# Message passing over 1.65 million edges on one core: some source rows fetched row by row on two other engines, and node transfers for four blocks

## The chip, the core and the metric

The kernel runs on one core of a Trainium2 chip. A core has five engines that take their own instructions in order: TensorE (PE in the profile; its weight loads are PEld), VectorE (DVE), ScalarE (ACT), GpSimd (POOL) and SyncE (SP), and 16 DMA engines that move data on their behalf. They meet through semaphores. The metric is the time of one execution on the device, in microseconds (us), lower being better.

## The reference

Nodes have 160 features (64 scalars, 32 vectors of three), edges four numbers; the edges are sorted by target.

```python
N, E = 50000, 1650000          # 2 x 800000 edges and a loop at each node
x   : [N, 160] f32             # node features
src, dst : [E] int32           # dst ascending
sh  : [E, 4] f32               # e0 = sh[:, :1], e1 = sh[:, 1:4]

s, v = x[:, :64], x[:, 64:].reshape(N, 32, 3)
ss, vv = s[src], v[src]                                        # gather of source rows
dot  = einsum('eui,ei->eu', vv, e1)
out0 = C0 * (ss * e0 @ W1 + dot * INV3 @ W2)
out1 = C1 * (p3 + p4 + p5)     # products of ss, vv with e0, e1 and W3, W4, W5
m    = concat([out0, out1])
h    = segment_sum(m, dst, N)  # then linear maps Ws, Wv
return layernorm(x + (x + relu(h)))
```

Every message is bilinear in the source's 160 features and the edge's four numbers, so the kernel first sums, for each target and each of the four edge numbers, the products with the source features, and applies the weights to the sums.

## The kernel before

**Units, groups, pairs.** The kernel takes most edges in units of 128. A unit needs the 128 source rows of `x` (640 bytes each), one on each partition: POOL fetches them with one indirect DMA (`gather`, L386) into a slot of `xg`. Six units are a group (`G`), three groups a "pair" of 18 units (`PG`), seven pairs a superchunk `s` (`SG` = 21 groups). `xg` has a tile for a pair, in four buffers, so POOL can be at most four pairs ahead of PE.

For each pair DVE makes `ha` (`spread`, L395 and L398): for each edge a one-hot of its target within a window of 32 nodes, times the four edge numbers, 128 x 128 a unit. PE multiplies `ha` by the unit's `xg` (`group_sums`, L423), six units adding up in one third of a PSUM tile `ps`. DVE turns `ps` over (`turn_sums`, L435) and adds the three groups into `ring` (L444), where a segment of four blocks of 128 nodes collects its sums. A kernel of 12,516 such units results.

**Blocks.** When the last group of a block of 128 nodes is past, PE multiplies its sums in `ring` by the weights (`block`, L756, five matmuls into `phb`), DVE adds relu of it to the node rows `xt` (L763) and takes mean and variance `mv` (L766, L768), ACT takes the root (`do_root`, L845, `rstd`), DVE inverts and applies it (`do_store`, L851 and L854), and SP stores the result (`do_send`, L862). `ahead` loads `xt` (L688). These steps come 1, 2, 3 and 4 pairs after the block's last group; two blocks (`BP`) share tiles and transfers.

**Own loops and packs.** The edges whose target is their source come as "own" rows in order of nodes (`ask_own`, L720 and L721, `set_own`). The others, without these, are rewritten to memory as `edges` in 16 `pack`s: DVE sorts out 128 long rows, and SP stores them row by row (`put`, L662), 18.9 KB of `edges` and 512 bytes of `selves` at addresses from registers, which one load of 16 numbers (L645) brings. `load` (L260) fetches a superchunk's edges on SP.

**Order.** SP, PE, DVE and ACT do things in the order in which the code is written (`manual_schedule`), and the loop over the pairs writes it: in each of the 18 unit steps of a pair it issues the unit's matmul, then `work(1.0)` takes waiting tasks from a queue that `after_pair` fills, then pack steps that are due. POOL has the gathers alone, in order.

Of the kernel before, what the change touches and what calls it, by code (L numbers as in the profile page):

```python
# [70 lines left out]
HEAD = 63  # L71
BP = 2
SB = 4
RP = 128
RS = 16
KM = 31
AHEAD = 3
SUMS = 3

def plan(n_nodes, n_edges):  # L80
# [24 lines left out]
def tile_gnn_resnorm(ctx: ExitStack, tc: tile.TileContext, x, src, dst, attr, W1, W2, W3, W4, W5, Ws, Wv, out, n_edges):  # L105
# [120 lines left out]
    with tc.tile_pool(name="once", bufs=1) as once, tc.tile_pool(name="raw", bufs=2) as rawp, \  # L226
            tc.tile_pool(name="idx", bufs=2) as idxp, tc.tile_pool(name="rows", bufs=4) as rowp, \
            tc.tile_pool(name="hots", bufs=1) as hotp, tc.tile_pool(name="ops", bufs=AHEAD + 1) as op, tc.tile_pool(name="sums", bufs=2) as sump, \
            tc.tile_pool(name="ring", bufs=2) as ringp, tc.tile_pool(name="node", bufs=6) as np_, \
            tc.tile_pool(name="ahead", bufs=6) as aheadp, \  # L230
            tc.tile_pool(name="psC", bufs=1, space=PSUM) as psC, tc.tile_pool(name="psK", bufs=1, space=PSUM) as psK, \
            tc.tile_pool(name="psP", bufs=1, space=PSUM) as psP, tc.tile_pool(name="psA", bufs=SUMS, space=PSUM) as psA, \
            tc.tile_pool(name="psM", bufs=1, space=PSUM) as psM, ExitStack() as later_pools:

        spotp, ownp = (later_pools.enter_context(tc.tile_pool(name=name, bufs=bufs))
                       for name, bufs in (("spot", 3), ("own", 2)))
        extremes = once.tile([P, 2, NSC], F32, name="extremes")
# [6 lines left out]
        nc.vector.tensor_copy(slotsP, slots)  # L244
        shareP, sumP = bank[:, 3, 64:64 + NK], bank[:, 3, 96:96 + BP * P // W]

# [3 lines left out]
        def load(s):  # L250
# [130 lines left out]

        def gather(s, placed, u, n):

            xg = rowp.tile([P, PG * G, D], F32, name="xg")
            for j in range(n):
                tc.add_to_no_dep_group(f"gathered{s % 2}", nc.gpsimd.indirect_dma_start(  # L386
                    out=xg[:, j, :], out_offset=None, in_=x,
                    in_offset=bass.IndirectOffsetOnAxis(ap=placed[0][:, u + j:u + j + 1], axis=0)).ins)
            return [xg[:, j, :] for j in range(n)]

# [27 lines left out]
        def group_sums(p, rows, ha):  # L418

            ps = psA.tile([P, PG, D], F32, name="ps")  # L420
            fresh("ps")
            for j, xr in enumerate(rows):
                mm = nc.tensor.matmul(ps[:, j // G, :], ha[:, j].rearrange("p k w -> p (k w)"), xr,  # L423
                                      start=j % G == 0, stop=j % G == G - 1)
                if j % G == 0:
                    wrote("ps", mm)
                else:
                    written["ps"][-1].append(mm.ins)
                yield ps

# [243 lines left out]
        def rows_of(b):  # L674
            nb = min(P, N - b * P)
            return nb, slice(b * P, b * P + nb)

        def together(b):

            bs = list(range(b // BP * BP, min(nblocks, b // BP * BP + BP)))  # L680
            return bs if all(rows_of(i)[0] == P for i in bs) else [b]

        def ahead(bs):

            nb = rows_of(bs[0])[0]
            n0, n1 = rows_of(bs[0])[1].start, rows_of(bs[-1])[1].stop
            xt = aheadp.tile([P, BP, D], F32, name="xt")
            dq.dma_start(xt[:nb, :len(bs)], x[n0:n1, :].rearrange("(h n) d -> n h d", h=len(bs)))  # L688

            mv = np_.tile([P, BP, 2], F32, name="mv")  # L690
            return [(xt, mv, h) for h in range(len(bs))]

# [7 lines left out]
        def own_blocks(k):  # L700

            if min((k + 1) * S, N) <= row_start(0)[1][0]:
                return []
            return [list(range(b, min(b + BP, nblocks))) for b in range(k * SB, min((k + 1) * SB, nblocks), BP)]

        def ask_own(k, bs, got):
# [5 lines left out]
            m = n // nq  # L712
            assert nq <= BP * P // W
            xr = ownp.tile([P, BP * P // W, D], F32, name="xr")
            sa = ownp.tile([P, BP * P // W, NK], F32, name="sa")
# [28 lines left out]

        products = {}

        def block(b, xt, mv, h):
            nb, row = rows_of(b)
            k, c0 = b // SB, b % SB * P
            bs = together(b)  # L750
            if b == bs[0]:
                products[b] = psM.tile([P, BP, D], F32, name="phb", tag="misc")
                fresh("misc")
            ph = products[bs[0]]
            for i in range(ND):
                wrote("misc", nc.tensor.matmul(ph[:nb, h], ring[k][:, i, c0:c0 + nb], BWk[:, i, :],  # L756
                                               start=i == 0, stop=i == ND - 1))
                yield 1
            if b != bs[-1]:
                return  # L760
            n = len(bs)
            y = xt[:nb, :n]
            nc.vector.scalar_tensor_tensor(y, ph[:nb, :n], 0.0, y, op0=ALU.max, op1=ALU.add)  # L763
            st = np_.tile([P, BP, 6], F32, name="st")
            for i in range(n):
                nc.vector.bn_stats(st[:nb, i], y[:, i])  # L766
            for i in range(n):
                nc.vector.bn_aggr(mv[:nb, i], st[:nb, i])  # L768

# [40 lines left out]
        def after_pair(p, f, *args):  # L810
            later.setdefault(p, []).append((f, args))
# [19 lines left out]

        def do_ahead(b):
            bs = together(b)
            if b == bs[0]:
                of_nodes.update(zip(bs, ahead(bs)))

        def do_block(b):
            yield from block(b, *of_nodes[b])

        def do_root(b):  # L840
            bs = together(b)
            if b == bs[-1]:
                n, (_, mv, _) = rows_of(b)[0], of_nodes[b]
                rstds[b] = np_.tile([P, BP], F32, name="rstd")
                nc.scalar.activation(rstds[b][:n, :len(bs)], mv[:n, :len(bs), 1], AF.Sqrt, bias=eps_t[:n])  # L845

        def do_store(b):
            bs = together(b)
            if b == bs[-1]:
                n, rstd = rows_of(b)[0], rstds.pop(b)  # L850
                nc.vector.reciprocal(rstd[:n, :len(bs)], rstd[:n, :len(bs)])  # L851
                for i in bs:
                    xt, mv, h = of_nodes[i]
                    nc.vector.tensor_scalar(xt[:n, h], xt[:n, h], mv[:n, h, 0:1], rstd[:n, h:h + 1],  # L854
                                            op0=ALU.subtract, op1=ALU.mult)

        def do_send(b):
            bs = together(b)
            if b == bs[-1]:
                n0, n1 = rows_of(bs[0])[1].start, rows_of(b)[1].stop  # L860
                xt = of_nodes[b][0]
                dq.dma_start(out[n0:n1, :].rearrange("(h n) d -> n h d", h=len(bs)), xt[:rows_of(b)[0], :len(bs)])  # L862
                for i in bs:
                    of_nodes.pop(i)

        def do_cast(s):
            raws[s] = cast(raws[s])

        def do_place(s):
# [72 lines left out]
        for b, g in enumerate(last_of):  # L942
            p = g // PG
            after_pair(max(p - 2, START - 1), do_ahead, b)
            for d, f in ((1, do_block), (2, do_root), (3, do_store), (4, do_send)):
                after_pair(p + d, f, b)
        later_pools.enter_context(tc.manual_schedule(engines={ET.SP, ET.PE, ET.DVE, ET.Activation}))
        turning = None
        for p, (s, g, ng) in enumerate(pairs):
            if p % per == 0 and s + 1 < NSC:  # L950
                end = reach(s + 1)
                assert end <= 0 or rows_stored[0] == NR or end <= row_start(rows_stored[0])[0][0]
                raws[s + 1] = load(s + 1)
                after_pair(p + 1, do_cast, s + 1)
# [3 lines left out]
            rows = gather(s, placed[s], (g - s * SG) * G, ng * G)  # L958
            for j, ps in enumerate(group_sums(p, rows, has.pop(p))):
# [194 lines left out]
```

## Time and profile before

| What | us |
|---|---|
| median of 3 runs | 17,977.61 |
| lowest and highest | 17,968.24, 17,986.82 |
| profiled execution | 18,051.88 |
| its span | 18,050.1 |
| POOL busy | 11,879.3 (66%) |
| DVE busy | 6896.5 (38%) |
| PE busy, matmuls | 6694.7 (37%) |
| PE busy, weight loads (beside the matmuls) | 5671.3 (31%) |
| ACT busy | 166.1 (1%) |

Times in the profile count from the span's start. A row of a group of instructions names the line, the engine, the operation, what it writes and reads, and the count, then busy time and the mean of one in ns, then the idle time just ahead of them on that engine and what ended most of it; "issue" means that nothing which the profile shows was waited for, and "remote" a releaser that it can't name. A row of the waits has total us, number and the longest. A row in order of time has start, duration, engine, line, operation and, in brackets, the idle time before. SPq and ACTq are the issuing of DMAs by SP and ACT. Register moves and loads are not shown as busy.

### The profile page before, as it was taken

The page shows a single profiled execution, that of the slowest core. Times are in us where ns is not written, and L with a number is a line of the kernel's source. Part 1 is how long each engine was busy: PE and PEld are TensorE (multiplying, and loading weights), DVE is VectorE, ACT ScalarE, POOL GpSimd, SP SyncE. Part 2 cuts the span into 40 slices and gives each one's busy share as a digit, 9 for nine tenths or more (in the row PEclk, how much of TensorE's full clock was granted, in tenths as well). Part 3 has the DMA queues.
Part 4 walks back from the last instruction along what each step waited for, and adds up shares of the span by engine and source line. Part 5 has one row for each costly group of instructions (what it writes and reads, how often), then busy time and mean ns, then how long its engine had stood idle before and what let it go on. Part 6 is the DMA issues. An engine that isn't in the chain of part 4 may idle for free. (4 is left out here: it accounts for less than half of the span.)

```text
span 18050.1 us, 95184 instructions
## 1 busy us (share of the span) xinstructions
PE 6694.7 (37%) x28959; PEld 5671.3 (31%) x28960; DVE 6896.5 (38%) x9751; ACT 166.1 (1%) x269; POOL 11879.3 (66%) x12530
## 2 busy tenths in 40 slices
PE   2333333333333333333333333333333333333333
PEld 2233333333333333333333333333233332333333
DVE  4343424334243343434334343343424434334222
ACT  0000000000000000000000000000000000000000
POOL 6566666666666666666666666666666666666666
PEclk6566566666666566566665666666666566656566
DMA  2223232222322323232232322323233232232222
GB/s 69 71 72 80 69 83 69 76 77 74 79 73 73 79 71 82 69 81 70 72 81 71 82 70 73 79 71 81 71 78 77 70 78 72 74 78 71 75 70 66
DMA packets 847363, 1343.26 MB, mean 74 GB/s; under 512 B 259593, under 2 KB 613844, under 8 KB 842784
## 3 DMA queue, kind: packets, MB, share of 16 engines
q0 software_dynamic: 600768, 1026.11, 23.9%
q1 hardware_dynamic: 244812, 310.13, 5.4%
q8 instruction: 230, 3.77, 0.1%
q14 instruction: 289, 2.37, 0.0%
q10 hardware_dynamic: 1264, 0.88, 0.0%
HBM read 1264.17 MB, written 72.09 MB: 74 GB/s over the span
## 5 line engine op out<-in xcount | busy, mean ns | idle before, releaser
L386 POOL DMA_INDIRECT xg<-in_x,sources x12516 | 11873.9, 949 | 6128.1 <-issue 3694.8
L423 PE MATMUL ps<-xg,ha 128*128 128x160 f32 x25032 | 5964.7, 365 | 8758.1 <-issue 8327.5
L423 PEld LDWEIGHTS ps<-xg,ha 128*128 128x128 f32 x25032 | 4955.5, 241 | 9606.1 <-issue 9123.2
L435 DVE STREAM_TRANSPOSE sums<-ps 128x480 f32<-128x480 f32 x696 | 469.7, 675 | 8745.5 <-PE ps L423 4451.9
L756 PE MATMUL phb<-BWk,ring 128*128 128x160 f32 (+1 forms) x3910 | 1225.8, 381 | 2522.0 <-issue 1747.7
L398 DVE TENSOR_TENSOR ha<-hot,pk 128x2304 f32<-128x2304 f32 x696 | 1776.1, 2552 | 24.9 <-DVE hot L395 1.0
L756 PEld LDWEIGHTS phb<-BWk,ring 128*128 128x128 f32 (+1 forms) x3910 | 882.3, 250 | 2694.7 <-issue 2358.5
L444 DVE TENSOR_TENSOR ring<-ring,sums 128x160 f32 x2086 | 688.0, 330 | 338.5 <-issue 232.6
L763 DVE SCALAR_TENSOR_TENSOR xt<-phb,xt 128x320 f32<-128x320 f32 x196 | 95.1, 485 | 1650.7 <-remote 1056.7
L395 DVE TENSOR_TENSOR hot<-bank,rel 128x576 f32<-128x576 f32 x696 | 521.4, 749 | 0.2
L740 DVE STREAM_TRANSPOSE ring<-xr 128x1280 f32<-128x1280 f32 x192 | 475.4, 2476 | 6.7
L610 DVE COPY_PREDICATED prow<-marks,prow 128x4734 f32<-128x4734 int32 (+6 forms) x80 | 432.7, 5409 | 0.6
L610 DVE COPY_PREDICATED pra<-marks,pra 128x3156 f32<-128x3156 int32 (+6 forms) x80 | 294.4, 3680 | 0.0
L736 DVE TENSOR_TENSOR xr<-xr,bank 128x1280 f32<-128x1280 f32 x192 | 284.8, 1483 | 10.2 <-remote 1.9
L845 ACT ACTIVATE rstd<-mv,eps_t 128x2 f32<-128x2 f32 x196 | 58.0, 296 | 17599.7 <-DVE mv L768 9083.3
L441 DVE TENSOR_TENSOR ring<-ring 128x199 f32<-128x199 f32 (+20 forms) x485 | 150.7, 377 | 2.3
L854 DVE TENSOR_SCALAR xt<-xt,mv,rstd 128x160 f32<-128x160 f32 x391 | 129.2, 372 | 15.2 <-issue 3.6
L698 DVE MEMSET ring<- 128x1255 f32 (+2 forms) x97 | 109.8, 1131 | 20.6 <-issue 20.6
L766 DVE BATCH_NORM_STATS2 st<-xt 128x6 f32<-128x160 f32 x391 | 108.2, 318 | 8.5 <-DVE xt L763 1.1
L368 DVE STREAM_TRANSPOSE pk<-raw 128x512 f32<-128x512 f32 x100 | 104.0, 1040 | 3.8 <-DMA raw<-in_attr 3.8
L607 DVE COPY_PREDICATED_SCALAR hit<-marks,none 128x789 int32 (+6 forms) x80 | 87.4, 1093 | 3.2 <-DVE pri L605 0.4
L627 DVE TENSOR_REDUCE mine<-pra 128x128 f32<-128x3200 f32 (+1 forms) x16 | 88.2, 5510 | 0.2
(337 smaller groups left out, 1469.9 us busy)
## 6 DMA issues: line engine op xcount, KB each, us to landing
xg<-in_x,sources POOLq DMA_INDIRECT x12516
xr<-in_x SPq DMA_DIRECT2D x191, 640.0 KB
edges<-prow SPq DMA_DIRECT2D x2030, 18.5 KB
raw<-edges SPq DMA_DIRECT2D x97, 384.0 KB
selves<-mine SPq DMA_DIRECT2D x2028, 0.5 KB
xt<-in_x SPq DMA_DIRECT2D x195, 160.0 KB
out<-xt SPq DMA_DIRECT2D x195, 160.0 KB
pra<-in_attr SPq DMA_DIRECT2D x15, 1580.0 KB
```

The source lines that it names most:

```text
L386: tc.add_to_no_dep_group(f"gathered{s % 2}", nc.gpsimd.indirect_dma_start(out=xg[:, j, :], out_offset=None, in_=x, in_offset=bass.Indirect ...
L395: nc.vector.tensor_tensor(hot[:, :n], slotsP[:, 0:W].unsqueeze(1).to_broadcast([P, n, W]), rel[:, u:u + n].unsqueeze(2).to_broadcast([P, n ...
L398: nc.vector.tensor_tensor(ha[:, :n], hot[:, :n].unsqueeze(2).to_broadcast([P, n, NK, W]), pk[:, :, u:u + n].rearrange("p k u -> p u k").un ...
L423: mm = nc.tensor.matmul(ps[:, j // G, :], ha[:, j].rearrange("p k w -> p (k w)"), xr, start=j % G == 0, stop=j % G == G - 1)
L435: nc.vector.transpose(at[:, :ng], ps[:, :ng].rearrange("p g (b f) -> p g b f", f=FB))
L441: nc.vector.tensor_tensor(ring[k][:, b, :past], ring[k][:, b, :past], ring[k - 1][:, b, S:S + past], op=ALU.add)
L444: nc.vector.tensor_tensor(here, here, at[:, i], op=ALU.add)
L610: nc.vector.copy_predicated(what[:n, a:e], mi[:, r].unsqueeze(2).to_broadcast([n, e - a, what.shape[2]]), what[:n, a + d:e + d])
L736: nc.vector.tensor_tensor(xr[:, :nq], xr[:, :nq], sumP[:, :nq].unsqueeze(2).to_broadcast([P, nq, D]), op=ALU.mult)
L740: nc.vector.transpose(ring[k][:, :, c0:c0 + nq * W].rearrange("p b (w q) -> p q b w", q=nq), xr[:, :nq].rearrange("p q (b f) -> p q b f", ...
L756: wrote("misc", nc.tensor.matmul(ph[:nb, h], ring[k][:, i, c0:c0 + nb], BWk[:, i, :], start=i == 0, stop=i == ND - 1))
L854: nc.vector.tensor_scalar(xt[:n, h], xt[:n, h], mv[:n, h, 0:1], rstd[:n, h:h + 1], op0=ALU.subtract, op1=ALU.mult)
```

## The change

Two engines take units from POOL. `ALONE` names for each: every how many pairs, at which remainder, and how many rows in a unit step. From pair 21 to pair 687 the second-last unit of every third pair is fetched by ACT and the last unit of every fourth pair by SP, each as 128 DMAs of one row of 640 bytes (`ask_alone`): eight loads of 16 addresses from `where` (which `address` makes on DVE once a superchunk) into registers, and for each row a register move and a DMA. Asking begins four pairs ahead (`LEAD`), three rows a unit step on ACT and two on SP. Their tiles have three buffers for each engine. The rows count up semaphores of their own, 16 for each engine, and PE waits for the whole unit just before its matmul. `gather` leaves these units out.

The other edits: `xt` and `out` move for four blocks in one DMA, 2560 contiguous bytes a partition in place of 640; a block's task does four blocks in two halves of two, with eight unit steps between; root, store and send come 3, 4 and 5 pairs after the last group. Own rows come for four blocks at once, in four DMAs of 32 partitions with four unit steps behind each. The edges of a superchunk are fetched in runs of 64 positions for two units each. `ha` is made two pairs ahead in place of three; the casts of a superchunk come in its third pair; fewer buffers for `xt` and own rows.

```diff
-BP = 2
+BP = 4
+AT = 2
+REST = 8
-AHEAD = 3
+AHEAD = 2
+ALONE = {"sync": (4, 1, 2), "scalar": (3, 0, 3)}
+LEAD = 4
+SEMS = 16
+AT_ONCE = 16
...
-                rows = what.rearrange("(u i q) -> i u q", u=P, i=NK)
-                dq.dma_start(to, rows)
+                rows = what.rearrange("(j i q) -> i j q", j=P // AT, i=NK)
+                dq.dma_start(to.rearrange("p (j t) q -> p j (t q)", t=AT), rows)
...
+        def address(s, at, fd, ef, af):
+            where = wherep.tile([P, NK, W], I32, name="where")
+            clipped = where.bitcast(F32)
+            nc.vector.tensor_scalar(clipped, ef[:, 0], 0.0, float(N - 1), op0=ALU.max, op1=ALU.min)
+            nc.vector.tensor_scalar(where, clipped, 4.0 * D, None, op0=ALU.mult)
+            where_of[s] = where, at[0]
+
+        def ask_alone(name, p):
+            s, g, ng = pairs[p]
+            where, u0 = where_of[s]
+            back = 1 + [n for n in ALONE].index(name)
+            u = u0 + (g - s * SG + ng) * G - back
...
+            to = alonep.tile([P, D], F32, name=f"alone_{name}")
+            sem, uses = kept[name][asked[name] % SEMS], asked[name] // SEMS + 1
...
+            came[p, back] = to, sem, uses * 16 * P, group
+            for i in range(NK):
+                for h in range(0, W, AT_ONCE):
+                    _, v = nc.values_load_multi_w_load_instructions(
+                        where[i * W + u // NK:i * W + u // NK + 1, u % NK, h:h + AT_ONCE], engines=[kind],
+                        min_val=0, max_val=(N - 1) * 4 * D, skip_runtime_bounds_check_because="clipped")
+                    for k in range(AT_ONCE):
+                        e = i * W + h + k
+                        d = eng.dma_start(to[e:e + 1, :].bitcast(U8), xbytes[ds(v[k], 4 * D)].rearrange("(o f) -> o f", o=1))
+                        d.then_inc(sem, 16)
...
+                        yield
...
             for j in range(n):
+                if n - j in alone:
+                    continue
...
+                alone = came.pop((p, len(rows) - j), None)
+                if alone:
+                    _, sem, count, group = alone
+                    tc.declare_fence(nc.tensor.wait_ge(sem, count).ins, group=group)
...
-            dq.dma_start(xt[:nb, :len(bs)], x[n0:n1, :].rearrange("(h n) d -> n h d", h=len(bs)))
+            dq.dma_start(xt[:nb, :len(bs)], x[n0:n1, :].rearrange("(n h) d -> n h d", h=len(bs)))
...
-                dq.dma_start(xr[:, :nq].rearrange("p q d -> p (q d)"), mine.unsqueeze(0).to_broadcast([NK, W, nq * D]))
                 dq.dma_start(sa[:, :nq].rearrange("p q k -> p (q k)"),
                              shares.unsqueeze(0).to_broadcast([NK, W, nq * NK]))
+                for part in range(NK):
+                    dq.dma_start(xr[part * W:(part + 1) * W, :nq].rearrange("p q d -> p (q d)"), mine)
+                    yield REST / 2
...
-            for d, f in ((1, do_block), (2, do_root), (3, do_store), (4, do_send)):
-                after_pair(p + d, f, b)
+                for d, f in ((1, do_block), (3, do_root), (4, do_store), (5, do_send)):
+                    after_pair(p + d, f, bs)
...
+        to_ask = {name: deque(p for p in range(3 * per, len(pairs) - 2 * LEAD) if p % every == at)
+                  for name, (every, at, _) in ALONE.items()}
...
                 work(1.0)
+                for name, of in to_ask.items():
+                    if name not in asking and of and of[0] - LEAD <= p:
+                        asking[name] = ask_alone(name, of.popleft())
+                    for _ in range(ALONE[name][2]):
+                        if name in asking and next(asking[name], 0) == 0:
+                            del asking[name]
```

The programs of three engines show where the rows stand. ACT before, from one pack to the next; `prow` and `marks` belong to the pack, `rstd` is the root of a block's variance, "x11" eleven instructions alike in a row:

```order
L526 CAST prow<-pri 128x790
L527 CAST prow<-pri 128x791
L528 COPY prow<-pra 128x790x4
L845 ACTIVATE rstd<-mv,eps_t 128x2
L546 CAST marks<-pri 128x790
L845 ACTIVATE rstd<-mv,eps_t 128x2 x11
```

ACT with the change, at the root of four blocks:

```order
L416 TENSOR_LOAD where
L421 DMA alone_scalar<-in_x 1x640 x14
L894 ACTIVATE rstd<-mv,eps_t 128x4 [waits DVE_49]
L421 DMA alone_scalar<-in_x 1x640 x2
L416 TENSOR_LOAD where
L421 DMA alone_scalar<-in_x 1x640 x16
```

Where ACT had a dozen instructions between packs, a root now stands behind and ahead of row DMAs.

SP before, while a pack is stored; the wait for DMAHW is that for the DMA eight ahead on SP, the wait for DVE that for the finished blocks:

```order
L662 DMA edges<-prow 1x18960 [waits DMAHW7_49]
L662 DMA selves<-mine 1x512 [waits DMAHW0_49]
L688 DMA xt<-in_x 128x2x160 [waits DMAHW1_49]
L862 DMA out<-xt 128x2x160 [waits DMAHW2_49,DVE_49]
L645 TENSOR_LOAD spots
L662 DMA edges<-prow 1x18960 [waits DMAHW3_49]
```

SP with the change, at such a place:

```order
L715 DMA edges<-prow 1x18960 [waits DMAHW0_49]
L715 DMA selves<-mine 1x512 [waits DMAHW1_49]
L906 DMA out<-xt 128x640 [waits DMAHW2_49,DVE_49]
L741 DMA xt<-in_x 128x640 [waits DMAHW3_49]
L416 TENSOR_LOAD where [waits DVE_49]
L421 DMA alone_sync<-in_x 1x640 [waits PE_sequencer_49,PE_49]
L421 DMA alone_sync<-in_x 1x640 x15
L416 TENSOR_LOAD where
L421 DMA alone_sync<-in_x 1x640 x4
L698 TENSOR_LOAD spots
L715 DMA edges<-prow 1x768 [waits DMAHW4_49]
```

The rows of `alone_sync` come between the stored rows, wait for no earlier DMA, and only the first for PE, which must be done with the buffer.

PE with the change, at the end of a pair whose last unit SP fetches (before, all 18 units of a pair read `xg` as the first rows do; DMASW is POOL's gathers):

```order
L474 MATMUL ps_141604<-xg_141586,ha_141036 128x160 [waits DMASW2_49]
L474 MATMUL ps_141604<-xg_141586,ha_141036 128x160 [waits DMASW3_49]
L474 MATMUL ps_141604<-alone_sync_140396,ha_141036 128x160 [waits own_sync13,PE_sequencer_49]
L474 MATMUL ps_141844<-xg_141825,ha_141404 128x160 [waits DMASW4_49,DVE_49,PE_49]
L474 MATMUL ps_141844<-xg_141825,ha_141404 128x160 [waits DMASW5_49]
```

Here PE stands until all 128 rows have landed, and the next pair's matmuls stand behind that.

More of the change, by code (lines that the diff above doesn't have):

```diff
@@ L388, in gather @@
                     in_offset=bass.IndirectOffsetOnAxis(ap=placed[0][:, u + j:u + j + 1], axis=0)).ins)
-            return [xg[:, j, :] for j in range(n)]
+            return [alone[n - j] if n - j in alone else xg[:, j, :] for j in range(n)]
         def spread(placed, u, n):
@@ L428, in group_sums @@
                     written["ps"][-1].append(mm.ins)
+                if alone:
+                    tc.declare_no_dep(mm.ins, group=group, reason="TensorE has waited for the semaphore of these rows")
                 yield ps
@@ L847, in do_store, with do_ahead @@
[L847 to L864, printed above, removed]
+        def do_ahead(bs):
+            of_nodes[bs[0]] = ahead(bs)
@@ L866, in do_cast, with do_send @@
+        def do_send(bs):
+            n0, n1 = rows_of(bs[0])[1].start, rows_of(bs[-1])[1].stop
+            xt, _ = of_nodes.pop(bs[0])
+            dq.dma_start(out[n0:n1, :].rearrange("(n h) d -> n h d", h=len(bs)), xt[:rows_of(bs[0])[0], :len(bs)])
         def do_cast(s):
             raws[s] = cast(raws[s])
+            address(*raws[s])
         def do_place(s):
@@ L957, in tile_gnn_resnorm @@
                     after_pair(p + 6, read_flags)
-            rows = gather(s, placed[s], (g - s * SG) * G, ng * G)
+            if p % per == 2 and s + 1 < NSC:
+                do_cast(s + 1)
+            rows = gather(s, placed[s], (g - s * SG) * G, ng * G, {b: came[p, b][0] for b in (1, 2) if (p, b) in came})
             for j, ps in enumerate(group_sums(p, rows, has.pop(p))):
```

103 lines of the change are left out of this document (56 added, 47 removed).

## The prediction

> **What bounds the kernel now.** I read the page first, then what GpSimd (POOL) waits for, then its gathers in order of time, and then the other engines in the same stretches. From the page:
>
> ```profile
> span 18050.1 us, 95184 instructions
> PE 6694.7 (37%) x28959; PEld 5671.3 (31%) x28960; DVE 6896.5 (38%) x9751; ACT 166.1 (1%) x269; POOL 11879.3 (66%) x12530
> L386 POOL DMA_INDIRECT xg<-in_x,sources x12516 | 11873.9, 949 | 6128.1 <-issue 3694.8
> L435 DVE STREAM_TRANSPOSE sums<-ps 128x480 f32<-128x480 f32 x696 | 469.7, 675 | 8745.5 <-PE ps L423 4451.9
> ```
>
> POOL does one thing, 12,516 gathers (L386), one for each unit of 128 edges. Its busy time and the idle time before it, 11,873.9 + 6128.1 = 18,002 us, fill the span, so the program lasts as long as POOL takes: 18,002 / 12,516 = 1.438 us a gather. The 696 transposes are one for each pair of 18 units. The idle time has two parts:
>
> ```profile
> POOL xg L386 <- issue: 3694.8, 12115, 1.7
> POOL xg L386 <- PE ps L423: 1516.8, 225, 94.6
> POOL xg L386 <- remote: 759.3, 138, 9.7
> POOL xg L386 <- PE phb L756: 151.1, 23, 7.1
> ```
>
> About 0.30 us stands before nearly every gather. The rest, some 2430 us, is in 386 waits for an `xg` buffer that TensorE (PE) still reads. In order of time:
>
> ```profile
> 8703.06 0.94 POOL L386 DMA_INDIRECT xg<-in_x,sources  x1 [0.30 <-issue]
> 8704.30 0.94 POOL L386 DMA_INDIRECT xg<-in_x,sources  x1 [0.30 <-issue]
> 8705.55 0.94 POOL L386 DMA_INDIRECT xg<-in_x,sources  x1 [0.30 <-issue]
> 8712.73 0.94 POOL L386 DMA_INDIRECT xg<-in_x,sources  x1 [6.24 <-PE ps L423]
> ...
> 8756.71 0.95 POOL L386 DMA_INDIRECT xg<-in_x,sources  x1 [0.30 <-issue]
> 8763.97 0.94 POOL L386 DMA_INDIRECT xg<-in_x,sources  x1 [6.31 <-PE ps L423]
> ```
>
> Gathers start every 1.25 us; after 36 of them POOL stands for some 6.3 us, then goes on: 51.2 us for 36 units. Why PE, busy 37%, is late shows in the stretches of each engine (busy time and count of PE matmuls, PE weight loads, DVE, ACT, POOL; then granted clock, DMA share, GB/s):
>
> ```profile
> 9012.00:9044.00 32.00, 5.66 (x14) 3.46 (x13) 0.00 (x0) 0.00 (x0) 22.85 (x25) 0.50 0.28 69
> 9044.00:9060.00 16.00, 11.63 (x67) 10.85 (x67) 10.18 (x17) 0.00 (x0) 8.61 (x9) 0.78 0.30 71
> 9048.96:9100.46 51.50, 17.71 (x83) 14.97 (x83) 12.64 (x23) 0.30 (x1) 34.21 (x37) 0.60 0.29 71
> 9409.99:9461.25 51.26, 20.58 (x91) 16.74 (x91) 20.24 (x28) 0.30 (x1) 34.24 (x37) 0.60 0.24 58
> 9425.00:9455.00 30.00, 5.92 (x14) 4.02 (x14) 6.15 (x7) 0.30 (x1) 22.69 (x24) 0.50 0.28 66
> ```
>
> While gathers run back to back, PE gets 27 or 28 instructions into 30 to 32 us, more than 1 us each, with neither data nor a buffer missing. Around a pause of POOL it does 134 in 16 us. The same two paces show on SyncE (SP), where each stored row is one register move and one DMA, as every row of the change will be:
>
> ```profile
> 8737.64 0.70 SPq L662 DMA_DIRECT2D edges<-prow  x1
> ...
> 8742.58 0.69 SPq L662 DMA_DIRECT2D edges<-prow  x1
> 8745.41 0.69 SPq L662 DMA_DIRECT2D selves<-mine  x1
> 8748.21 0.69 SPq L662 DMA_DIRECT2D edges<-prow  x1
> ...
> 8763.61 0.00 SPq L662 DMA_DIRECT2D selves<-mine  x1
> ...
> 8776.56 0.00 SPq L662 DMA_DIRECT2D selves<-mine  x1
> ...
> 8790.62 0.01 SPq L662 DMA_DIRECT2D selves<-mine  x1
> ...
> 8970.42 0.22 SPq L662 DMA_DIRECT2D edges<-prow  x1
> 8970.73 0.22 SPq L662 DMA_DIRECT2D selves<-mine  x1
> 8971.05 0.22 SPq L662 DMA_DIRECT2D edges<-prow  x1
> ```
>
> In a pause a row takes 0.32 us; under running gathers it takes up to 2.8. From 8737.64 to 8790.62 there are 32 rows: 15 in the 13 us from 8763.61 to 8776.56, behind a pause, and 17 in the other 40 us, 2.35 us each. So the bound is POOL's issue of gathers, lengthened by a PE that is slow while POOL issues. Any engine that issues DMAs row by row meets the second fact.
>
> **The change part by part.** The sum is made against the profiled execution, 18,051.88 us (span 18,050.1), 0.41% above the median 17,977.61; the last step goes to the median by x 0.9959.
>
> *Gathers removed.* Pairs 21 to 687 lose one unit in every third pair (223, to ScalarE, ACT) and one in every fourth (167, to SP): 390 gathers. If all else kept up, this saves 390 x 1.25 = 488 us (its own issue) to 390 x 1.438 = 561 us (pauses shrinking in proportion).
>
> *Rows added.* 223 x 128 = 28,544 row DMAs on ACT and 21,376 on SP, each with its move, and 8 register loads a unit. What these queues hold now:
>
> ```profile
> edges<-prow SPq DMA_DIRECT2D x2030, 18.5 KB
> selves<-mine SPq DMA_DIRECT2D x2028, 0.5 KB
> 92.70 1.80 ACTq L175 DMA_DIRECT2D BWk<-BVd  x4
> ACT rstd L845 <- DVE mv L768: 9083.3, 96, 132.2
> SPq L862 <- DVE xt L854: 3893.9, 54, 119.6
> xt<-in_x SPq DMA_DIRECT2D x195, 160.0 KB
> out<-xt SPq DMA_DIRECT2D x195, 160.0 KB
> 8832.04 0.41 SPq L862 DMA_DIRECT2D out<-xt  x1
> PE ps L423 <- DVE ha L398: 16.3, 1, 16.3
> ```
>
> SP has 4058 stored rows, 23 in 72 units. With 128 rows added it must issue 151 in 72 units, which now last 103.6 us. After the change their 69.8 gathers take 87.2 us at 1.25. With one fast stretch in it SP issues 15 rows there and 74 / 2.35 = 32 in the rest: 47. PE reaches the unit that is not complete and waits, POOL fills its four buffers and stops, and then rows go at 0.32 us: 104 x 0.32 = 33 us. So 72 units take 87 + 33 = 120.6 us instead of 103.6, +16.4%. Pairs 21 to 687 are 667 of 696, so +15.7%: 20,890 us.
>
> ACT has issued no DMA under running gathers; its nearest own row is the four above, 0.45 us each, before the gathers press. Its cost there lies between nothing (128 rows at 0.45 are 58 us, less than the 65.4 us that 52.3 gathers take) and the pace of SP. By SP's pace, 54 units (now 77.7 us) hold 15 + 52.4 / 2.35 = 37 of the 128 rows; 91 are left at 0.32, 29 us: 94.5 us, +21.6%, over the 667 pairs +20.7%: 21,790 us. With 0.45 for the rows left it would be +35%, 24,440 us. SP's rows are the nearest to ACT's, the same two instructions in the same stretch, so I take its pace. The pauses of the two engines fall partly together; I take the middle of 20,890 and 21,790, 21,340, which on the median's scale is **21,250 us**.
>
> *Queues behind the rows.* ACT's square roots (L845 before) now stand among its rows. Today ACT is there long before its data. Once ACT is late, DVE's reciprocal waits for it, behind that the transposes and the `ha` of the next pairs, and PE with them. So ACT cannot lag by four pairs, which is the lead of its rows, and PE pays earlier; not more, because the rows left are the same. On SP the edge loads and the `out` stores stand between rows; the 3893.9 us that `out` waits for DVE is slack of a queue with nothing else to do, and turns into row time. It does not help above, where SP issues without a stop.
>
> *PE's waits.* At most 390 more instructions on PE. At the slow pace of 1.1 us that is 430 us of an engine that then stands waiting anyway; taken as nothing, at most +2.4%.
>
> *Transfers for four blocks, edges in runs of 64, quadrants, fewer buffers, `address`.* Of 390 `xt` and `out` DMAs half go, at 0.41 us each 80 us of SP's queue; three quadrant loads more for each segment of four blocks give a third of that back, and `address` adds two small operations per superchunk on DVE. The block matmuls are the same, in halves of two blocks. SP's queue and DVE, 38% busy, cover all this; without that cover it is at most 80 us either way. Of one `ha` buffer fewer I expect nothing: PE waits for `ha` once now, 16.3 us.
>
> [...]
>
> **Rivals.** *The rows are hidden: faster.* For it: the cycle with 30 stored rows in it (9048.96:9100.46, 51.50 us) is no longer than the one without any (9409.99:9461.25, 51.26), so row DMAs hardly hinder POOL; and ACT is idle. Against it: the pace of SP. It needs ACT at 65.4 / 128 = 0.51 us a row and SP at 87.2 / 151 = 0.58, against 2.35 outside the fast stretch. Then 18,052 - 488 to 18,052 - 561, or 17,490 to 17,420 on the median's scale; 17,455. It turns into a loss where rows average more than about 0.8 us under running gathers: the 13.6 us that POOL now idles in 72 units hold 42 rows, and 109 are left for 87.2 us.
>
> *The slow pace is milder*, 1.2 us a row, because longer pauses bring more fast stretches and own rows wait for no earlier DMA, as the stored ones do. SP then issues 15 + 62 in 87.2 us, 74 are left, 24 us: 111 us, +6.8%, 19,200 us. Between this and no loss lies all that is slower and under the forecast's own range.
>
> *The saving is eaten by POOL's longer waits*: PE's work is unchanged, its pace sets how often POOL stops, and each gather less becomes 1.25 us more of waiting. Then 17,978 us and no difference. For it: 2430 us of such waits. Against it: PE's fast stretches follow the pauses, so that such a balance would have to be met by accident.
>
> [...]
>
> **How the numbers follow.** The forecast (19,200 to 22,900) has 0.46, above that (ACT's rows at 0.45 us) 0.07; slower but under 19,200, 0.10; no difference 0.05; hidden rows, 17,420 to 17,490, or a part of that gain, 0.32. Within 0.2% is what a measurement here can hardly tell from no change. The range over all runs from 17,420, the full saving, to 22,900, between ACT's two prices; the likeliest case's own is 19,200 to 22,900. Faster 0.32, same 0.05, slower 0.63.
>
> **What would show it.** 12,126 gathers. If right: pauses of POOL of 25 us and more, about one in 54 to 72 units, each behind a matmul that stands for `alone` rows; row DMAs on SP and ACT at over 2 us in the gathers' stretch and near 0.32 us in a pause; gathers still 1.25 us apart. Wrong: ACT's rows 0.6 us apart or less beside running gathers, POOL's pauses no longer than now, and about 17.5 ms. If only ACT keeps pace, the loss is SP's and near 20,800 us. If POOL's own gathers come more than 1.25 us apart, the row DMAs collide with them, which I left out.

## The result and the profile after

The changed kernel took 23,999.67 us (23,978.79 to 24,105.91), the kernel before 17,976.02 beside it: ratio 1.336, interval 1.3344 to 1.3376. Slower was right; the size was not, and 24,000 us lies above the range, whose upper end was 22,900.

Two of the later sets of runs met a condition in which the kernel before takes 15,715 us in place of 17,980, and there the change is *faster*, by 2.3%; kernels are therefore compared only where the kernel before took the same time beside them.

From the page of the changed kernel:

```profile
span 23976.9 us, 197983 instructions
PE 6023.0 (25%) x28959; PEld 5544.1 (23%) x28960; DVE 6833.2 (28%) x9468; ACT 139.2 (1%) x172; POOL 11494.4 (48%) x12140
L433 POOL DMA_INDIRECT xg<-in_x,sources x12126 | 11489.1, 947 | 12422.2 <-PE ps L474 6179.5
L474 PE MATMUL ps<-alone_sync,ha 128*128 128x160 f32 x334 | 139.7, 517 | 7223.4 <-PEq L473 6607.7
L474 PE MATMUL ps<-alone_scalar,ha 128*128 128x160 f32 x446 | 160.2, 450 | 4557.1 <-PEq L473 3945.0
alone_scalar<-in_x ACTq DMA_DIRECT2D x28544, 0.6 KB
alone_sync<-in_x SPq DMA_DIRECT2D x21376, 0.6 KB
```

The 390 gathers are gone and one still takes 947 ns, but the idle time ahead of them has grown from 6128 to 12,422 us. PE's few matmuls on `alone` rows carry 7223 + 4557 us of waiting, nine tenths of it in its own queue at L473, the wait for the rows. POOL's waits:

```profile
POOL xg L433 <- PE ps L474: 6179.5, 254, 88.2
POOL xg L433 <- issue: 5452.9, 11695, 80.1
POOL xg L433 <- remote: 771.8, 166, 12.1
```

Before, PE's row here had 1516.8 us and 94.6 at the longest. The "issue" row is in the main the 0.3 us ahead of each gather, 3557 us in all; the other 1900 us are stops, up to 80 us long, for which the trace names no releaser. One stop, in order of time; first POOL:

```profile
12085.30 0.94 POOL L433 DMA_INDIRECT xg<-in_x,sources  x1 [73.31 <-PE ps L474]
12086.55 0.95 POOL L433 DMA_INDIRECT xg<-in_x,sources  x1 [0.30 <-issue]
...
12171.53 0.94 POOL L433 DMA_INDIRECT xg<-in_x,sources  x1 [0.30 <-issue]
12246.32 0.94 POOL L433 DMA_INDIRECT xg<-in_x,sources  x1 [73.84 <-PE ps L474]
```

and in it the rows' two engines and PE (a merged row has the start of its first instruction and the time to the end of its last):

```profile
12100.93 58.80 ACTq L421 DMA_DIRECT2D alone_scalar<-in_x  x22
12145.72 25.20 SPq L421 DMA_DIRECT2D alone_sync<-in_x  x10
12182.13 62.91 ACTq L421 DMA_DIRECT2D alone_scalar<-in_x  x144
12234.74 15.11 SPq L421 DMA_DIRECT2D alone_sync<-in_x  x36
12239.20 0.90 PE L474 MATMUL ps<-alone_sync,ha 128*128 128x160 f32 x2 [150.53 <-PEq L473]
12239.90 10.50 PE L474 MATMUL ps<-xg,ha 128*128 128x160 f32 x68
```

POOL issues 70 gathers in 87.5 us, then stands 73.8 us. While it issues, ACT takes 58.80 / 22 = 2.7 us a row and SP 25.20 / 10 = 2.5; while it stands, 62.91 / 144 = 0.44 and 15.11 / 36 = 0.42. PE stands 150 us at the unit that SP hasn't finished, and then does 68 matmuls in 10.5 us. That is the mechanism forecast. This stop of 74 us is one of the long ones: by the trace POOL is idle for more than 20 us at a stretch 160 times (before once), 41 us on average and 38 in the median, where the sum had 33.

### The profile page after: what moved, and what is told of

Its sections match the earlier page's. It is cut to its first block, busy times and chain, and to the rows that moved or that the text cites. A ratio compares the mean times of both kernels' runs of the same rounds, so it can differ in the third digit from the quotient of the medians.

```text
span 23976.9 us, 197983 instructions
## 1 busy us (share of the span) xinstructions
PE 6023.0 (25%) x28959; PEld 5544.1 (23%) x28960; DVE 6833.2 (28%) x9468; ACT 139.2 (1%) x172; POOL 11494.4 (48%) x12140
## 3 DMA queue, kind: packets, MB, share of 16 engines
q14 instruction: 1090, 8.93, 0.1%
## 5 line engine op out<-in xcount | busy, mean ns | idle before, releaser
L433 POOL DMA_INDIRECT xg<-in_x,sources x12126 | 11489.1, 947 | 12422.2 <-PE ps L474 6179.5
L474 PE MATMUL ps<-xg,ha 128*128 128x160 f32 x24252 | 5130.3, 354 | 5101.0 <-issue 4746.9
L474 PEld LDWEIGHTS ps<-xg,ha 128*128 128x128 f32 x24252 | 4561.4, 236 | 5413.0 <-issue 5065.7
L474 PE MATMUL ps<-alone_sync,ha 128*128 128x160 f32 x334 | 139.7, 517 | 7223.4 <-PEq L473 6607.7
L474 PEld LDWEIGHTS ps<-alone_sync,ha 128*128 128x128 f32 x334 | 82.6, 300 | 7285.0 <-PEq L473 6657.9
L812 PEld LDWEIGHTS phb<-BWk,ring 128*128 128x128 f32 (+1 forms) x3910 | 1095.0, 322 | 1056.1 <-issue 489.0
L474 PE MATMUL ps<-alone_scalar,ha 128*128 128x160 f32 x446 | 160.2, 450 | 4557.1 <-PEq L473 3945.0
L474 PEld LDWEIGHTS ps<-alone_scalar,ha 128*128 128x128 f32 x446 | 98.1, 265 | 4609.2 <-PEq L473 3987.2
L795 DVE STREAM_TRANSPOSE ring<-xr 128x2560 f32<-128x2560 f32 x96 | 430.0, 4479 | 3.3
L791 DVE TENSOR_TENSOR xr<-xr,bank 128x2560 f32<-128x2560 f32 x96 | 270.1, 2814 | 542.2 <-DMA xr<-in_x 533.0
```

What stands on the lines that cost most here:

```text
L791: nc.vector.tensor_tensor(xr[:, :nq], xr[:, :nq], sumP[:, :nq].unsqueeze(2).to_broadcast([P, nq, D]), op=ALU.mult)
L795: nc.vector.transpose(ring[k][:, :, c0:c0 + nq * W].rearrange("p b (w q) -> p q b w", q=nq), xr[:, :nq].rearrange("p q (b f) -> p q b f", ...
L812: wrote("misc", nc.tensor.matmul(ph[:nb, h - h0], nodes, BWk[:, i, :], start=i == 0, stop=i == ND - 1))
```

## The experiments

Ratios are to the kernel before in the same set. Lines of code below are those of the changed kernel.

**Without rows; one engine's rows; one DMA for a unit's rows.** `ALONE = {}`; `{"scalar": (3, 0, 3)}`; `{"sync": (4, 1, 2)}`; and, in place of the eight loads and the 128 moves and row DMAs,

```diff
-            for i in range(NK):
-            ...
+            d = eng.dma_start(to, x[p * P % (N - P):p * P % (N - P) + P, :])
+            d.then_inc(sem, 16)
```

> The changed kernel with ALONE = {}: POOL gathers all 12,516 units, everything else of the change stays. Theory A (the loss is that of the row DMAs, which ACT and SP can't issue fast enough): as before, 17,980 within 80 us. Theory B (part of the loss lies in the transfers for four blocks, the later root and store, or the fewer buffers): clearly above 18,100 us.

> ALONE keeps ScalarE alone (every third pair, its last unit). Theory A: per 54 units the gathers take 65.4 us, in which ACT issues at the profile's mean of 0.80 rows per us 52 rows; 76 are left at 0.42 us (0.34 a row and a register load of 1.33 us for each 16), 32 us, and PE needs some 5 us to catch up: 102 us in place of 77.7 in 96% of the program, 22,000 to 23,400 us. Theory C (DVE's waits for ACT's square root, 4118 us in the changed kernel, carry the loss, not the rows): the same here, but then SP alone costs nothing. Theory D (the two engines' losses add): this and SP alone exceed 17,980 by amounts that sum to 6000.

> ALONE keeps SyncE alone (every fourth pair, its last unit). Theory A: per 72 units 87.2 us of gathers hold 0.69 x 87 = 60 of SP's 151 rows; 91 are left at 0.42, 38 us, with PE's catching up 130 us in place of 103.6: 21,600 to 22,500 us. Theory C: ACT is free, no DVE wait, so 17,500 to 18,000 us. Theory D: with ScalarE alone it adds up to 6000 us over 17,980; if the pauses are shared instead, each alone is nearly as slow as both, above 22,500.

> Both engines ask for their units as in the changed kernel, but with one DMA of 128 contiguous rows in place of 128 row DMAs (other rows than the sources, so the sums are not the reference's). Theory A: with the rows gone the removed gathers come back in full or nearly, 17,400 to 17,520 us. Theory E (PE's pace sets how often POOL stops, so that fewer gathers only lengthen the stops): 17,900 to 18,050 us.

Before took 17,979.13 us. Measured: without rows 18,378.58 (1.0237, 1.0212 to 1.0262); ACT's rows alone 23,526.15 (1.3083); SP's alone 23,040.77 (1.2817); one DMA a unit 17,962.13 (0.9996, 0.9976 to 1.0016).

The row DMAs cost 24,000 - 17,962, some 6000 us, since with one DMA in their place nothing of it is left. The 17,962 us lie in theory E's range and miss theory A's 17,400 to 17,520, since neither knew what the other edits cost. Against the kernel without rows the removed gathers do come back: 18,379 - 17,962 = 416 us of the 488 to 561 forecast, so theory E falls. The two engines' losses don't add: 5150 us for ACT and 4660 for SP over the kernel without rows, 5620 for both. Their stops are shared, and theory D falls. SP alone loses nearly as much though ACT is free, against theory C. Theory A's figures for one engine were 0.1 to 0.5 thousand too low at their upper ends. What theory A did not have: the edits beside the rows cost 400 us, so theory B's figure came true; the cause, found below, is none of those that it names.

**What in a row costs time.** `AT_ONCE = 32`; rows at fixed addresses, in place of the loads, moves and row DMAs (the first cut below); the root taken off ACT (the second, which leaves the square root out):

```diff
+            for e in range(P):
+                r = p * P % (N - P) + e
+                d = eng.dma_start(to[e:e + 1, :], x[r:r + 1, :])
```

```diff
-            nc.scalar.activation(rstds[bs[0]][:n, :len(bs)], mv[:n, :len(bs), 1], AF.Sqrt, bias=eps_t[:n])
+            nc.vector.tensor_scalar(rstds[bs[0]][:n, :len(bs)], mv[:n, :len(bs), 1], EPS * HALF * HALF, None, op0=ALU.add)
```

> The changed kernel with AT_ONCE = 32: four register loads of 32 addresses for a unit in place of eight of 16. In the profile of the changed kernel one load takes 1.33 us in a pause, 10.6 us for a unit, which the prediction's sum left out. Theory A (the engines' instruction time for the rows sets the pauses): with loads of the same length 5 us less for each of the 390 units, of which those of one engine at a time count: 22,800 to 23,600 us. Theory F (loads are hidden): 23,900 to 24,100.

> The changed kernel with each row's DMA at an address known when the program is built (other rows than the sources): the same 49,920 row DMAs, without their register moves and loads, so half the instructions. Theory A (each instruction takes a turn of up to 1.4 us under running gathers): the pace in rows doubles there, 72 units hold 115 to 140 of SP's 151 rows while gathers run, 18,400 to 20,500 us. Theory G (the DMAs are the limit, not the instructions around them): 23,000 to 24,000 us.

> The changed kernel with the square root of the variance left out: DVE adds the small constant itself and ACT issues only rows (and the casts of the packs). Theory A: what DVE waited for there is time in which PE stands for rows anyway, 23,500 to 24,100 us. Theory C (the wait of DVE for ACT's root, 4118 us in the changed kernel, holds up the sums and PE): below 22,500 us.

Before took 17,979.96 us, within 4 us of the sets that this one is compared with. Loads of 32: 23,781.63 (1.3213, 1.3191 to 1.3235); fixed addresses 20,295.72 (1.1295); no root 23,617.22 (1.3132). The same 49,920 row DMAs without moves and loads cost 3700 us less: the instructions around the DMAs make most of the loss, as theory A has it, and theory G falls. Counted as for the changed kernel further below, a row beside running gathers then takes 0.93 us on SP and 0.79 on ACT in place of 1.46 and 1.24, so the pace does not double, as theory A said, but rises by a good half. These rows are also neighbours in memory; what that alone does was not tried. Loads of 32 save only 218 us, which lies between the ranges of theories A and F: one takes 2.2 us in a stop, not 1.33, so a unit's loads go from 10.6 to 8.8 us. Without the root the loss shrinks by 382 us, less than a tenth, so theory A holds here and C falls once more. DVE's row for this wait in the changed kernel,

```profile
DVE rstd L898 <- ACT rstd L894: 4117.8, 58, 129.9
```

is ten times what taking the wait away gave back: a wait's total isn't its price.

**Few rows.** `ALONE = {"scalar": (9, 0, 2)}`.

> ALONE keeps ScalarE alone and every ninth pair, 74 units, two rows a unit step. Base is the kernel without rows, 18,379 us. Theory A: 162 units last some 235 us, in which ACT needs 128 / 0.88 = 145 us at the pace that it had beside running gathers: no pause is added, 74 gathers of 1.1 to 1.3 us go: 18,280 to 18,300 us. Theory H (any row DMAs lengthen the stops, by their turns or by the root behind them): 18,400 us or more.

18,706.25 us (1.0410, 1.0392 to 1.0427), 328 us above the kernel without rows, so H was right on the sign and A's sum wrong. The rows are asked four pairs ahead of PE, which is 103 us at 1.43 us a unit; by the trace the 128 rows of one of the 74 units take 176 us from first to last (median; 123 to 310). What PE's matmuls on these rows waited for:

```profile
  PEq L473: 732.9, 28
  issue: 642.8, 65
  DMA alone_scalar<-in_x: 203.0, 7
```

In 28 of 74 units PE stood at L473 for rows, 26 us each. So the lead was too short, though the mean rate, 128 rows in the 238 us of nine pairs, was enough. That the lead decided is argued, not shown: a longer one was tried only in the other condition (below), and how much of the 328 us it would save is open.

**Where 400 us beside the rows come from.** In the kernel without rows, DVE and POOL at the end of one of the longer stops:

```profile
9084.11 0.25 DVE L315 TENSOR_SCALAR sources<-bank 128x126 int32<-128x126 f32 x1
9085.13 0.94 POOL L433 DMA_INDIRECT xg<-in_x,sources  x1 [15.94 <-PE ps L474]
```

`sources` are the indices for a superchunk's gathers. DVE makes them in `place`, which the loop calls `AHEAD` pairs before the end of a superchunk; `AHEAD` from 3 to 2 put it one pair later, where POOL, four pairs ahead of PE, is already waiting for it. The bracket names PE, which the profile infers from the semaphore events that it has; that POOL really stood for `sources` is read from the times, and tested below. Counted in the traces, POOL's first gather after `sources` comes within 1.5 us of it, out of a stop, in 56 of 100 superchunks, and in none before the change. The mending edit makes all but `pk` a pair earlier (its other part, not shown, moves `pk` to the end of `place`):

```diff
+                    if (p + AHEAD + 1) % per == per - 1 and s + 1 < NSC:
+                        parting = do_place(s + 1)
+                        for _ in range(3):
+                            next(parting)
                     if (p + AHEAD) % per == per - 1 and s + 1 < NSC:
-                        for _ in do_place(s + 1):
+                        for _ in parting:
```

> The kernel without rows (18,379 us), with the making of a superchunk's `sources` on DVE one pair earlier, where it stood before the change (only the transposed edge numbers `pk` stay where they are). In the profile without rows POOL resumes within 1.5 us of `sources` in 56 of 100 superchunks, in pauses of 13 us; before the change in none. Theory S (the 400 us come from AHEAD 3 to 2, which put `sources` a pair later, so that POOL, four pairs ahead, waits for them): 17,950 to 18,050 us. Theory B (transfers, halves, later root and store): 18,300 to 18,400.

> The changed kernel with all its rows, and `sources` one pair earlier. Theory A (POOL's long stops are the rows' time, and where they end with `sources` DVE was only late because PE stood for rows): the 400 us at most, 23,500 to 24,000 us. Theory I (the late `sources` multiply with the rows: 3695 us of the changed kernel's stops end with them): under 22,000 us.

> `sources` early; ScalarE alone fetches the last unit of every seventh pair, 95 units, and asks nine pairs ahead, so that it has some 230 us for 128 rows in place of 103. Theory A: at 0.6 to 0.88 rows per us, 145 to 215 us are enough, no stop is added, 95 gathers of 1.1 to 1.3 us go: 105 to 125 us below the early kernel without rows, so 17,850 to 17,880 if that is 17,980. Theory H (row DMAs cost whatever their lead, by the turns that they take from PE): above that kernel.

> `sources` early; one DMA of 128 contiguous rows for each of the 390 units (other rows than the sources). The saving of POOL's issue if the rows cost nothing: 416 us below the early kernel without rows, as with late sources (18,379 to 17,962), up to 488: 17,490 to 17,570. If POOL's stops fill up what is saved: 17,900 or more.

The set met the other condition: before took 15,714.72 us (15,710.88 to 15,717.81). Early `sources` without rows 15,733.83 (1.0012, 1.0003 to 1.0021); with all rows 15,358.89 (0.9773, 0.9758 to 0.9788); ACT's rows in every seventh pair, nine pairs ahead, 15,618.47 (0.9938); one DMA a unit 15,249.73 (0.9704, 0.9691 to 0.9717). None of the absolute figures expected holds. Within the set, ACT's units (93, not the 95 expected) save 115 us, as theory A had it, their last row 160 us and more ahead of PE, and 390 in one DMA each save 484 us, the 488 of gathers 1.25 us apart. Rows in their place keep 375 of these.

**The kernels again, to part program from condition.**

> The changed kernel itself once more. The runs so far fall in two sorts of chip: where the kernel before takes 17,980 us, and one where it takes 15,715, with nothing in the program different. Theory K (the slow pace of PE, SP and ACT under running gathers belongs to the chip that runs the program, and decides the sign of the change): where before takes 15,715, 15,330 to 15,450 us, faster by 1.7 to 2.4%; where it takes 17,980, again 24,000. Theory L (the third set was fast because its kernels make `sources` early): 24,000 or 18,000 on either, or far above the early kernel with rows on this chip.

> No rows, late `sources`. Theory K: where before takes 15,715, PE is close behind POOL, DVE makes `sources` in time in any case, 15,700 to 15,760 us; where it takes 17,980, again 18,380.

> No rows, early `sources`. Where before takes 17,980 us: theory S 17,950 to 18,050, theory B 18,300 to 18,400 (as expected for this kernel the first time). Where it takes 15,715: 15,734 as the first time.

> All rows, early `sources`. Where before takes 17,980 us: theory A 23,500 to 24,000, theory I (late `sources` multiply with the rows) under 22,000. Where it takes 15,715: 15,359 as the first time, and by theory K the changed kernel within 60 us of it.

Before took 18,055.65 us. The changed kernel 24,160.27 (1.3378, 1.3356 to 1.3400); no rows 18,532.13 (1.0275, 1.0250 to 1.0300); no rows with early `sources` 18,093.09 (1.0021, 1.0011 to 1.0030); all rows with early `sources` 23,534.81 (1.3037). So the late `sources` cost 439 of the 476 us that the edits beside the rows cost here (theory S); 37 us, 0.2%, are left for all the others. With rows they cost 625 us, more than the 400 that theory A allowed; its figure came true even so, and theory I falls.

**Last set.**

```diff
-            xg = rowp.tile([P, PG * G, D], F32, name="xg")
+            xg = rowp.tile([P, PG * G, D // 4], F32, name="xg")
...
-                    out=xg[:, j, :], out_offset=None, in_=x,
+                    out=xg[:, j, :], out_offset=None, in_=x.rearrange("n (a b) -> (n a) b", a=4),
```

> No rows, early `sources`, and every gather fetches 128 rows of 160 bytes in place of 640 (from the first quarter of `x`, so the sums are not the reference's); PE reads each four times over, so that its matmuls and the instructions of all engines keep their number and shape. Where before takes some 18,000 us: theory M (the bytes of the gathers slow the other engines' instructions) near 15,700 us, without stops of POOL; theory N (the number of gathers and of their packets does) 17,900 to 18,150, as with whole rows. Where before takes 15,715: 15,700 by both.

> The changed kernel a third time, for the chance of a chip on which before takes 15,715 us. Theory K (the pace of that chip decides the sign): there 15,330 to 15,450 us; where before takes some 18,000, again 24,000 to 24,200.

Before took 15,711.56 us, so the quarter rows (15,707.98) tell nothing on bytes against number; that stays open. The changed kernel itself took 15,351.82, ratio 0.9769, 0.9753 to 0.9786: theory K, as far as it says that the condition decides the sign, and theory L falls. That the condition belongs to the *chip* is not borne out: the records give this set the same chip number as the first two, where before took 17,980.

What it looks like there, from its page, PE's and POOL's waits, and the two row engines in the same 30 us beside running gathers:

```profile
span 15359.6 us, 197983 instructions
PE 10553.0 (69%) x28959; PEld 6876.2 (45%) x28960; DVE 6886.4 (45%) x9468; ACT 138.8 (1%) x172; POOL 11509.5 (75%) x12140
L433 POOL DMA_INDIRECT xg<-in_x,sources x12126 | 11504.2, 949 | 3824.5 <-issue 3502.2
PE ps L474 <- DMA xg<-in_x,sources: 4625.4, 7707, 7.6
POOL xg L433 <- PE ps L474: 90.9, 269, 2.6
8999.80 22.53 ACTq L421 DMA_DIRECT2D alone_scalar<-in_x  x54
9009.87 18.48 SPq L421 DMA_DIRECT2D alone_sync<-in_x  x48
```

The program is the same to the instruction, and a gather takes as long. But PE follows POOL so closely that it waits for gathers to land, POOL's long stops are gone (3502 of 3824 us of its idle time are the 0.3 us between gathers), and rows take 22.53 / 54 = 0.42 us on ACT and 18.48 / 48 = 0.39 on SP with POOL issuing. Three possible causes of the two conditions find no support in these two traces. The granted clock of PE is not higher here (0.569, and 0.597 where the kernel took 24,000 us). Transfers are not shorter: a packet of a gather takes 118 ns on average here and 115 there. And instructions are brought hardly faster: their two queues move the same 12.8 MB, in packets of 426 and 1090 ns here and of 444 and 1130 there.

One thing does differ: the trace holds 333,855 events of semaphores here and 118,906 where the kernel took 24,000 us. The same holds for one program in both conditions, that without rows and with early `sources`: 240,195 events at 15,734 us and 44,507 at 18,093. No run tells whether that goes with the cause or follows from the pace, so the cause of the two conditions stays open.

## Why the forecast was right and wrong

**What bounds the kernel: right for the condition it was read in.** POOL's issue, lengthened by stops for a PE that is slow while POOL issues. The forecast took the slow pace for a consequence of the gathers themselves. It is not: with the same gathers, 1.25 us apart, before takes 15,715 us, which is 12,516 x 1.25 = 15,645 and a little. The step "any engine that issues DMAs row by row meets the second fact" holds in one condition and not in the other.

**Gathers removed: nearly right.** 416 us in the slow condition and 484 in the fast one where a unit is one DMA, against 488 to 561.

**Rows added: mechanism right, the sum of the stops wrong.** The step that failed is "87 + 33 = 120.6 us instead of 103.6". Of the 103.6 us, 13.6 are stops that POOL has anyway; the sum let one stop for rows take their place. In the trace they stand beside it: POOL has 318 idle stretches of 2 to 20 us, 2303 us together or 13.7 us for 72 gathers, about as many as before (379, 2346 us) and without rows (321, 2548 us). These 2300 us are most of what the sum lacks, 23,977 - 21,340 = 2640 us in the profiled execution.

The stops for rows themselves came out near the forecast, with luck. The 160 idle stretches of more than 20 us hold 6577 us; the forecast's middle left 21,340 - 12,126 x 1.25 = some 6200 us for all stops. Two errors in it nearly cancel, and a third adds to them. First, more rows are issued beside running gathers than assumed. SP starts 9996 of its 26,643 DMAs in the 14,583 us in which gathers start at most 2 us apart, and 16,637 in the other 9343 us; ACT 11,731 and 16,813 of its 28,544 rows. Averaged over that time, a row takes 1.46 us on SP and 1.24 on ACT beside running gathers, better than the 1.86 (87.2 us for 47) and 1.77 (65.4 for 37) that the sum had. Second, a row in a stop costs more than 0.32 us: in the long stops SP issues 83 DMAs, nearly all of them rows, in 41 us on average, 0.49 us each, and ACT 85 rows, 0.48 each. A row with its move takes 0.34; the register load of 1.33 us for each 16 adds 0.08, and was mentioned in the forecast but not priced, 10.6 us a unit; the first 3 us of a stop (median), in which rows still come slowly, are part of the rest, which is not taken apart further. Third, some 620 us of the long stops belong to the late `sources`: the changed kernel's second run has 6802 us of them, with early `sources` 6178.

With the ordinary stops kept, the parts add up: 12,126 x 1.25 + 2303 + 6577 = 24,040, against a span of 23,977 us. That is bookkeeping of one trace, not a second test.

That the stops of the two engines overlap was right. Taking the middle of the two was not: over the kernel without rows both cost 5620 us, more than the dearer one alone (5150).

**Transfers, fewer buffers, `AHEAD`: the second failed step.** They were priced at nothing, or at most 80 us, with DVE's 38% as cover, and of `AHEAD` the `ha` buffer alone was looked at. `AHEAD` also sets when `place` runs, and with it when POOL has its next indices; that was in the code and in none of the waits of before, where POOL waited for `sources` 0.4 us in all. It cost 400 to 440 us without rows and 625 with them. It does not decide the miss: with early `sources` the changed kernel still takes 23,535 us, above the range. The transfers themselves cost no more than the 37 us that remain, as forecast.

**Queues behind the rows: nearly right.** The root behind ACT's rows made DVE wait for 4118 us, and taking it away gave back 382; the forecast had nothing.

**The rivals.** Hidden rows came true in the fast condition: it asked for 0.51 us a row on ACT and 0.58 on SP, and 0.42 and 0.39 were measured in the stretch above; it gained 2.3% rather than 2.9%. The point from which it should turn, 0.8 us, lies between these and the 1.24 and 1.46 of the slow condition. The eaten saving (17,978) did not occur. The milder rival's pace, 1.2 us a row, was nearer to the measured 1.46 and 1.24 than the sum's own, but its 19,200 us did not come: it too put the stop's rows at 0.32 us and left the ordinary stops out. The upper case with 0.07, 24,440 us from ACT's 0.45 us a row in a stop, came nearest; the range stopped short of it. Its price was about right (0.48), its time in part luck, since it had ACT's pace beside gathers too slow and the ordinary stops at nothing.

Of the signs given, the gathers (12,126, 1.25 us apart), the matmuls that stand for rows and the slow rows beside gathers came. Stops of 25 us and more came 138 times, one in 88 gathers, rarer than the one in 54 to 72 forecast.

## What to carry to other kernels

Before work is moved to an idle engine, price it at the pace that this engine's instructions have *beside* the bottleneck, all of them, moves and register loads too: idle 99% of the time says nothing of that pace. When a sum adds a new wait, keep the waits that are there already, unless something shows that the new one takes their place. When a constant is lowered to free memory, look for every place that reads it; here one that was taken for a buffer count also decided when the bottleneck's next indices were ready. And a time belongs to the condition in which it was measured: the same instructions were 34% slower and 2.3% faster than before, so measure both kernels side by side, more than once.

## What the runs showed of the hardware

That there are two conditions for one program on one core, constant within a set of runs: before at 17,976 to 18,056 us or at 15,712 to 15,715. In the first, PE, SP and ACT started an instruction about every 0.6 to 1.4 us while indirect gathers were issued (27 PE instructions in 32 us, a row of two instructions 1.24 to 2.8 us), and row DMAs sped up to 0.42 us some 3 us after the gathers stopped; in the second, rows took 0.39 and 0.42 us beside gathers. A register load of 16 numbers took 1.33 us and one of 32 took 2.2, so that half as many loads saved 1.8 us a unit and 218 us in all.
